# Local-window attention on one Trainium2 core: smaller key tiles, one-pass scores from split operands, and a layer's activations kept in memory

## The chip, the cores and the metric

The kernel runs on one core of one Trainium2 chip. The metric is device time in microseconds (us) of one execution. Each execution of a run also has a span (first to last instruction) and a mean granted TensorE clock. In what follows PE is TensorE, PEld its weight loads, DVE is VectorE, ACT is ScalarE, POOL is GpSimd and SP is SyncE.

## The reference, cut to what matters

Four layers act on four images of 256 channels and 48x48 pixels, each of them with a group norm in front and a residual added. Layers 0 to 2 are convolutions that the change hardly touches. Layer 3 is attention without a softmax: each pixel sums over square windows of 48, 24 and 12 pixels around it.

```python
def _L3_conv_ref(x, Wq, Wk, Wv, Wout, bout):
    # 8 heads of 32 channels, WINDOWS = (1, 2, 4)
    q = sigmoid(einsum('bchw,oc->bohw', x, Wq)); k = sigmoid(... Wk)
    v = v / maximum(norm(v, axis=1), 1e-12)
    for w in WINDOWS:
        ws  = Hh // w
        wk  = _box(Ik, ws, Hh, Ww)        # sums of k over a ws x ws window
        wkv = _box(Ikv, ws, Hh, Ww)       # sums of k v^T over it
        attn = einsum('bdhw,bdfhw->bfhw', q, wkv)
        norm = einsum('bdhw,bdhw->bhw', q, wk)
        outs.append(attn / (norm[:, None] + 1e-06))
    return einsum('bchw,oc->bohw', concatenate(outs), Wout) + bout
...
x = x + _L3_conv_ref(_gn(x), ...)
```

## The kernel before

It computes scores q.k for a tile of 128 key pixels and a block of 8 query rows (384 pixels), multiplies them by a 0/1 mask for each of the three windows, and multiplies the masked scores by v with a column block of ones, so that rows 0 to 31 of an accumulator hold the numerator of a head and rows 32 to 63 its denominator. Two heads are done side by side. A key tile is 128 pixels in a row, that is 2 2/3 rows of the image, and sees all 48 columns.

```python
def attend(qk, vs, rb, ct, pr, o, norm):          # two heads, one block of 8 query rows
    accs = [ps_acc.tile([P, NB], F32, ...) for wi in range(NW)]   # one buffer each
    def scores(kt):
        s = ps_s.tile([P, 2, 512], F32, tag="s")                  # two buffers in all
        for j in range(2):
            g = (2 * pr + j) * D                                  # 32 rows of the array
            nc.tensor.matmul(s[:, j, 0 : (hi - lo) * W],
                qk["k", ct][g : g + D, kt * P : (kt + 1) * P],
                qk["q", ct][g : g + D, lo * W : hi * W], ...)     # fp32
    ahead = scores(todo[0][0])
    for i, kt in enumerate(todo[0]):
        s = ahead
        ahead = scores(next tile)
        for wi in range(NW):
            sm = smp.tile([P, 2, RB, W], F32, tag="sm")
            nc.vector.tensor_mul(sm[...], s[...], masks[...])     # DVE, line 700
            for j in range(2):
                nc.tensor.matmul(accs[wi][64 * j : 64 * (j + 1), ...],
                    vs[ct][:, kt, 2 * pr + j, :], sm[:, j, 0:n, :], ...)   # line 706
    for wi in range(NW):                                          # end of a head pair
        for j in range(2):
            g = (2 * pr + j) * D
            nc.scalar.copy(o[g : g + D, ct, wi, :], accs[wi][64 * j : 64 * j + D])
            nc.scalar.activation(norm[g : g + D, wi, :],
                accs[wi][64 * j + D : 64 * j + 2 * D], AF.Identity, bias=eps_sb[g : g + D])
...
for rb in range(NRB):
    for ct in range(NCT):
        for pr in range(HEADS // NCT // 2):
            attend(qk, vs, rb, ct, pr, o, norm)
            ...                                     # the previous block's output product
        nc.vector.reciprocal(norm, norm)            # line 761: 128 x 1152, all on DVE
        nc.vector.tensor_mul(o[:, ct], o[:, ct], norm)
```

The order of instructions on an engine is not quite that of the source: a scheduler orders them when the program is built.

## Time and profile before

| | before |
|---|---|
| time, median of the first 3 runs | 6971.76 us (6965.56 to 6979.1) |
| profiled span | 6986.8 us |
| mean granted clock | 0.905 |
| last convolution product of layer 2 ends | 2570 us |
| first score of layer 3 | 2660 us |

The page's busy times, groups, stretches and timeline are shown in the prediction below and are not repeated. Two lines of it matter later and were not shown there. They are groups of instructions, with count, then busy us and mean ns, then idle time of the engine just before them:

```profile
L718 ACT ACTIVATE norm<-acc,eps_sb 32x384 f32<-32x384 f32 x576 | 330.3, 573 | 7.2
L717 ACT COPY o<-acc 32x384 f32<-32x384 f32 x576 | 270.3, 469 | 3534.9 <-PE acc L706 3529.8
```

They are the evictions of the accumulators at the end of each of 96 head pairs: 12 small ScalarE operations, each of 32 of 128 partitions, 6.3 us in a row by their means. The accumulators have one buffer each, so the next head pair's products wait for them.

The granted clock over the span in 40 slices (in tenths; 9 is 0.9 or more) shows where the clock is lost. It is mostly layer 3, which begins in slice 15 of 40 (mean 0.87 from 2600 us on); slices 14 and 15 lie largely in layer 2:

```profile
PEclk9999999999999889988889988888898888988888
```

### The profile page before, as it was taken

What the parts mean: (1) busy time and instruction counts of PE and PEld (TensorE: products, weight loads), DVE (VectorE), ACT (ScalarE), POOL (GpSimd) and SP (SyncE); (2) the same over time, 40 slices, a digit from 0 to 9 for tenths busy, and PEclk for the clock granted to TensorE, in tenths of its full rate; (3) what the DMA queues carried; (4) which work ended last, traced back from release to release, by engine and by line L of the source; (5) the groups of instructions that cost most, each with busy time, mean ns of one, the idle gap of its engine ahead of it and who ended that gap; (6) DMA issues with size and microseconds to landing.
All of it is one profiled execution on the core that took longest, in us unless ns stands there. A gap on an engine that the chain in (4) does not pass through costs nothing.

```text
span 6986.8 us, 63861 instructions
## 1 busy us (share of the span) xinstructions
PE 6467.4 (93%) x27732; PEld 2934.3 (42%) x27732; DVE 3257.0 (47%) x4210; ACT 841.5 (12%) x1687; POOL 72.4 (1%) x146
## 2 busy tenths in 40 slices
PE   7999999999999879899989999989899999999998
PEld 3555555455555544333334333334333334333333
DVE  1201110101010216766666776666776665777666
ACT  0000000000000002111112111112111112111111
POOL 0000000000000000000000000000000000000000
PEclk9999999999999889988889988888898888988888
DMA  2000000000000120000000000000000000000000
GB/s 104 9 9 9 7 29 8 6 15 25 5 11 16 9 60 14 5 5 5 5 5 19 5 5 5 5 5 19 5 5 5 1 5 5 10 3 3 5 5 5
DMA packets 100436, 84.81 MB, mean 12 GB/s; under 512 B 70043, under 2 KB 94651, under 8 KB 96443
## 3 DMA queue, kind: packets, MB, share of 16 engines
q1 hardware_dynamic: 89595, 59.85, 3.6%
q10 hardware_dynamic: 10416, 17.44, 0.7%
q0 software_dynamic: 144, 3.43, 0.2%
q8 instruction: 218, 3.57, 0.2%
q14 instruction: 63, 0.52, 0.0%
HBM read 61.37 MB, written 22.75 MB: 12 GB/s over the span
## 4 chain that ended last, share of the span: by engine, by line
PE 88%; DVE 6%; ACT 3%; issue 2%; DMA 2%; SPq 0%; POOL 0%; POOLq 0%; ACTq 0%; DVEq 0%
PE acc L706 29%; PE cv L339 22%; PE s L675 18%; PE cv L462 10%; DVE norm L761 3%; PE out_ps L734 3%; DVE sm L700 2%; PE proj_ps L599 2%; ACT norm L718 1%; PE ap L442 1%; ACT o L717 1%; PE v_ps L621 1%; DMA xn<-x_d 0%; DMA w_sb<-in_w_dram 0%; PE sum_ps L295 0%
## 5 line engine op out<-in xcount | busy, mean ns | idle before, releaser
L700 DVE TENSOR_TENSOR sm<-s,masks 128x768 f32<-128x768 f32 (+7 forms) x3152 | 2439.4, 819 | 1083.6 <-PE s L675 1060.4
L706 PE MATMUL acc<-sm,v 128*64 128x384 f32 (+7 forms) x12608 | 2290.7, 492 | 364.1 <-DVE sm L700 295.6
L706 PEld LDWEIGHTS acc<-sm,v 128*64 128x64 f32 x12608 | 838.4, 148 | 1934.0 <-issue 1114.6
L339 PE MATMUL cv<-pad,w_sb 128*128 128x480 f32 (+1 forms) x3920 | 1579.6, 561 | 0.2 <-DVE pad L318 0.2
L675 PE MATMUL s<-q,k 32*128 32x384 f32 (+5 forms) x5760 | 1448.5, 572 | 10.9 <-DVE sm L700 10.9
L339 PEld LDWEIGHTS cv<-pad,w_sb 128*128 128x128 f32 x3920 | 737.4, 190 | 790.2 <-issue 731.1
L675 PEld LDWEIGHTS s<-q,k 32*128 32x128 f32 x5760 | 501.8, 204 | 660.3 <-issue 610.5
L462 PE MATMUL cv<-pad,wl_sb 128*128 128x384 f32 (+1 forms) x2592 | 712.1, 438 | 4.6 <-DVE pad L176 3.2
L717 ACT COPY o<-acc 32x384 f32<-32x384 f32 x576 | 270.3, 469 | 3534.9 <-PE acc L706 3529.8
L363 DVE TENSOR_TENSOR e<-lg,bn_inv 120x196 f32<-120x196 f32 (+1 forms) x20 | 7.2, 358 | 967.7 <-PE lg L360 967.7
L462 PEld LDWEIGHTS cv<-pad,wl_sb 128*128 128x128 f32 x1728 | 327.3, 190 | 234.4 <-issue 5.5
L761 DVE RECIPROCAL norm<-norm 128x1152 f32<-128x1152 f32 x48 | 352.7, 7347 | 46.5 <-ACT norm L718 46.5
L718 ACT ACTIVATE norm<-acc,eps_sb 32x384 f32<-32x384 f32 x576 | 330.3, 573 | 7.2
L499 DVE SCALAR_TENSOR_TENSOR x<-cv,alpha,x 128x384 f32<-128x384 f32 x48 | 29.6, 617 | 527.5 <-PE cv L462 527.5
L348 ACT ACTIVATE k<-cv,b_sb 128x480 f32<-128x480 f32 (+1 forms) x20 | 12.9, 645 | 2050.4 <-PE cv L339 2050.4
L734 PE MATMUL out_ps<-o,wout_sb 128*128 128x384 f32 x576 | 223.6, 528 | 14.8 <-DVE o L762 14.1
L164 DVE COPY gn_m<-gn_ps 128x2 f32<-128x2 f32 x16 | 2.5, 157 | 371.9 <-PE gn_ps L163 371.6
L734 PEld LDWEIGHTS out_ps<-o,wout_sb 128*128 128x128 f32 x576 | 106.7, 198 | 112.1 <-issue 40.6
L442 PEld LDWEIGHTS ap<-seen,xT 120*128 120x128 f32 (+2 forms) x832 | 115.7, 219 | 18.4 <-ACT seen L435 11.5
L452 DVE TENSOR_TENSOR x<-x,ap 128x240 f32<-128x240 f32 (+1 forms) x80 | 27.0, 391 | 197.7 <-PE ap L442 197.7
L442 PE MATMUL ap<-seen,xT 120*128 120x120 f32 (+3 forms) x832 | 117.5, 304 | 1.1 <-ACT seen L435 0.8
L462 PEld LDWEIGHTS <-wl_sb 128*128 128x128 bf16 x864 | 87.0, 101 | 65.3 <-issue 10.5
(108 smaller groups left out, 1316.7 us busy)
## 6 DMA issues: line engine op xcount, KB each, us to landing
rows<-band_d SPq DMA_DIRECT2D x64, 168.8 KB, 3.0
x<-in_x_dram SPq DMA_DIRECT2D x8, 1152.0 KB, 7.7
x_d<-x SPq DMA_DIRECT2D x8, 1152.0 KB, 4.1
res<-x_d SPq DMA_DIRECT2D x24, 384.0 KB, 3.2
xn<-x_d SPq DMA_DIRECT2D x8, 1152.0 KB, 7.4
out_dram<-res ACTq DMA_DIRECT2D x24, 384.0 KB, 2.5
w_sb<-in_w_dram ACTq DMA_DIRECT2D x14, 448.0 KB, 6.3
masks<-in_masks_dram POOLq DMA_DIRECT2D x1, 3348.0 KB, 25.9
```

Source lines behind the costliest of these rows:

```text
L339: nc.tensor.matmul(ps, w1_sb[:, ct, t, :], pad[:, ct, :, r0 : r0 + nr, c0 : c0 + HP], start=(n == 0), stop=(n == NCT * T0 - 1),)
L442: nc.tensor.matmul(pf[:, f, a:e], xTs[k + i][:n, f, mo * P : (mo + 1) * P], seen[:n, 1 + i, a:e], start=(i == 0), stop=(i == near[-1]),)
L462: nc.tensor.matmul(ps, w_sb[:, ct, t, mo * P : (mo + 1) * P], pad[:, ct, r0 : r0 + RB, c0 : c0 + W], start=(n == 0), stop=(n == NCT * T1 - 1),
L599: nc.tensor.matmul(ps, proj[name][:, ct, mo * P : (mo + 1) * P], xf[:, ct, rb * NB : (rb + 1) * NB], start=(ct == 0), stop=(ct == NCT - 1),)
L621: nc.tensor.matmul(ps, xf[:, ct, kt * P : (kt + 1) * P], proj["v"][:, ct, :], start=(ct == 0), stop=(ct == NCT - 1),)
L675: nc.tensor.matmul(s[:, j, 0 : (hi - lo) * W], qk["k", ct][g : g + D, kt * P : (kt + 1) * P], qk["q", ct][g : g + D, lo * W : hi * W], sta ...
L700: nc.vector.tensor_mul(sm[:, :, 0:n, :], s[:, :, (a - lo) * W : (z - lo) * W].rearrange("p j (r w) -> p j r w", w=W), masks[:, ph, at : at ...
L706: nc.tensor.matmul(accs[wi][64 * j : 64 * (j + 1), (a - rb * RB) * W : (z - rb * RB) * W], vs[ct][:, kt, 2 * pr + j, :], sm[:, j, 0:n, :], ...
L717: nc.scalar.copy(o[g : g + D, ct, wi, :], accs[wi][64 * j : 64 * j + D])
L718: nc.scalar.activation(norm[g : g + D, wi, :], accs[wi][64 * j + D : 64 * j + 2 * D], AF.Identity, bias=eps_sb[g : g + D],)
L734: nc.tensor.matmul(ps, wout_sb[:, kt, mo * P : (mo + 1) * P], o[:, kt % NCT, kt // NCT, :], start=(kt == 0), stop=(kt == NW * NCT - 1),)
L761: nc.vector.reciprocal(norm, norm)
```

## The change

Its intent: make the scores cheaper (each q and k is split into a high and a low half, the four combinations are stacked in 128 rows, and one float32r product replaces a true fp32 one), make the windows tighter (a key tile is 8x16 pixels, so the small windows need only part of the columns), take the wide reciprocal apart (numerators and denominators go through memory, so 24 reciprocals of 128x72 replace 48 of 128x1152), and let the projections of the next image run in the background. In windows where a part of the mask is all ones, ScalarE copies that part and VectorE multiplies the rest.

```diff
+F32R = mybir.dt.float32r
+KC = P // RB                       # 16 columns: key tiles of 8x16 pixels
...
+kst = [kvp.tile([P, NKT, P], F32R, ...) for i in range(2 * NPR)]   # k: high, low, high, low
...
+nc.gpsimd.tensor_copy(hl[:, 0], t)                                  # high half
+nc.gpsimd.tensor_sub(hl[:, 1], t, hl[:, 0].bitcast(F32))            # low half
+nc.sync.dma_start(out=dst[...], in_=hl.bitcast(F32))                # q, k, v to memory
...
 def scores(a, c):
     for j in range(2):
         nc.tensor.matmul(
             s[:, j, 0 : (r1 - r0) * (c1 - c0)],
-            qk["k", ct][g : g + D, kt * P : (kt + 1) * P],
-            qk["q", ct][g : g + D, lo * W : hi * W],
+            kst[2 * pr + j][:, a * NKC + c, :],
+            qs[:, j, r0:r1, c0:c1],
...
+    pieces = [(c0, c1, True)]
+    if abs(a - rb) * RB + RB <= h:
+        f0, f1 = max(0, c * KC + KC - h), min(W, c * KC + h + 1)
+        if f0 < f1:
+            pieces = [(f0, f1, False), (c0, f0, True), (f1, c1, True)]
+    for p0, p1, masked in pieces:
+        if masked:
+            nc.vector.tensor_mul(dst, src, mask[wi][...])            # line 807
+        else:
+            nc.scalar.copy(dst, src)                                 # line 815
...
-            nc.scalar.copy(o[g : g + D, ct, wi, :], accs[wi][64 * j : 64 * j + D])
-            nc.scalar.activation(norm[g : g + D, wi, :], accs[wi][...], AF.Identity, bias=...)
+    if (a, c) == todo[wi][-1]:
+        nc.scalar.copy(stage[:, wi, :], accs[wi])                    # 128 rows at once
+nc.gpsimd.dma_start(out=o_d[b][rb, ...], in_=stage[...])             # and to memory
+nc.gpsimd.dma_start(out=n_d[b][rb : rb + 1, ...], in_=stage[...])
...
-        nc.vector.reciprocal(norm, norm)
-        nc.vector.tensor_mul(o[:, ct], o[:, ct], norm)
+    nc.vector.reciprocal(nr, nr)                                     # 128 x 72
```

The cut parts are the mask tables, the projections in blocks of rows, and the loop that runs the late steps (reciprocal, reload, output product) and the next image's projections between key tiles.

## The prediction

> **What bounds it now.** I read the page's busy times first, then its costliest groups, then the table of 20 us stretches over image 1's attention, then the timeline inside one stretch. The change touches layer 3 alone, which runs from about 2600 to 6987 us: 4387 us of the span.
>
> ```profile
> PE 6467.4 (93%) x27732; PEld 2934.3 (42%) x27732; DVE 3257.0 (47%) x4210; ACT 841.5 (12%) x1687; POOL 72.4 (1%) x146
> ...
> L700 DVE TENSOR_TENSOR sm<-s,masks 128x768 f32<-128x768 f32 (+7 forms) x3152 | 2439.4, 819 | 1083.6 <-PE s L675 1060.4
> L706 PE MATMUL acc<-sm,v 128*64 128x384 f32 (+7 forms) x12608 | 2290.7, 492 | 364.1 <-DVE sm L700 295.6
> ...
> L675 PE MATMUL s<-q,k 32*128 32x384 f32 (+5 forms) x5760 | 1448.5, 572 | 10.9 <-DVE sm L700 10.9
> ...
> L761 DVE RECIPROCAL norm<-norm 128x1152 f32<-128x1152 f32 x48 | 352.7, 7347 | 46.5 <-ACT norm L718 46.5
> ```
>
> PE is nearly always busy, and DVE waits for PE, not PE for DVE. That names PE, but a busy PE may be a slow one. The stretches (columns: stretch, length, PE, PEld, DVE, ACT, POOL, PE clock, DMA share, GB/s) show when:
>
> ```profile
> 4320.00:4340.00 20.00, 20.00 (x122) 8.09 (x122) 18.18 (x23) 0.16 (x1) 0.00 (x0) 1.00 0.00 1
> 4340.00:4360.00 20.00, 11.68 (x62) 4.45 (x62) 15.01 (x11) 6.08 (x12) 0.00 (x0) 0.88 0.00 1
> 4360.00:4380.00 20.00, 20.00 (x64) 6.34 (x64) 8.06 (x11) 0.00 (x0) 0.00 (x0) 0.50 0.00 0
> 4380.00:4400.00 20.00, 20.00 (x114) 7.98 (x112) 15.96 (x21) 1.30 (x3) 0.00 (x0) 0.94 0.00 1
> ```
>
> PE idles 8 us, then runs 20 us at half clock, issuing 64 matmuls instead of about 120. The timeline there names the cause:
>
> ```profile
> 4349.87 7.35 DVE L761 RECIPROCAL norm<-norm 128x1152 f32<-128x1152 f32 x1
> ...
> 4358.09 1.54 PE L706 MATMUL acc<-sm,v 128*64 128x384 f32 x4 [6.69 <-DVE sm L700]
> ```
>
> The wide reciprocal stands in front of the mask products, so PE waits 6.69 us. This happens 48 times. The third thing to read is a stretch without it:
>
> ```profile
> 4082.88 0.91 PE L675 MATMUL s<-q,k 32*128 32x384 f32 x4
> 4083.72 1.92 PE L706 MATMUL acc<-sm,v 128*64 128x384 f32 x12
> 4085.57 0.91 PE L675 MATMUL s<-q,k 32*128 32x384 f32 x4
> 4086.41 1.76 PE L706 MATMUL acc<-sm,v 128*64 128x384 f32 x12
> 4088.10 0.91 PE L675 MATMUL s<-q,k 32*128 32x384 f32 x4
> ```
>
> From start to start, a score group takes 0.84 us and the acc groups 1.85 and 1.69 us. Their windows have 1008 and 912 columns in the source, so 0.16 us buys 96 columns: 1.67 ns per column of a pair of heads, the two heads side by side. What is left is a fixed 0.17 us for an acc group and, at 384 columns, 0.20 us for a score group. The same two constants fit other steps.
>
> **The sum of layer 3 before**, at full clock. Counts come from the built program: scores 1,027,584 columns / 2 x 1.67 = 856 us; acc 2,022,912 / 2 x 1.67 = 1686; output, q/k and v products 221,184 x 1.67 = 369; 2917 changes of group x 0.18 = 525. That is 3436 us. The other 951 us are the reciprocals and what follows them (48 x about 17 = 800: 7 of idling, 10 lost at half clock), and some 150 us around the four projections.
>
> **What the skill says.** (1) "FP8 and Floating Point Precision", TensorE Precision Notes: true FP32 makes four passes through the array, reduced-precision FP32 is truncated to FP22. 1.67 ns is four cycles at the 2.4 GHz of "TensorE: Matmul & The Clock Gate", so the four passes agree; one pass for float32r no run here shows. (2) "TensorEngine Tiling (Array Packing)", Key Properties: "Changing tiling mode (not just tile) drains the TensorE". The trace agrees: 0.17 to 0.20 us at each change between 32-row and 64-column tiles. After the change scores use the whole array and acc still 64-column tiles, so this cost stays. (3) "TensorE: Matmul & The Clock Gate", the HAM clock gate: an idle window of about 3.4 us drops the clock to half. The trace agrees on 0.50, but it stays there some 20 us here. (4) "DMA: Bandwidth & Descriptors", Anatomy of one DMA: about 2.0 us fixed for a software DMA. The kernel before has one such issue, of 3348 KB (25.9 us), which doesn't test it.
>
> **The change, part by part.**
> - *Scores.* Four 32-row copies (k high/low by q high/low) fill 128 rows, so one pass replaces four, but the heads no longer run side by side. Tiles of 8x16 pixels see at most 40 columns at the edges: 970,752 columns x 0.417 ns = 404 us instead of 856. Gain 452.
> - *Acc.* 1,716,800 columns instead of 2,022,912: 1431 us, gain 255. In the new order 226 products stand apart from their partner; half of them pay again, about 0.5 us each: +57.
> - *Changes of mode* 3310 x 0.18 = 596: +71. Output and projections unchanged, 369.
> - *DVE.* A product costs about 1.04 ns per element plus 0.105 us (2439 us for 3152 products with 2,022,912 elements). Now 4032 products, 1,171,520 elements: 1220 + 423 = 1643 us. The wide reciprocals become 24 of 72 columns. With o<-o,rc (48 x 1.35), evictions and small ops: some 1820 us, against 2857 of PE.
> - *ACT* gets 1440 unmasked copies (0.3 to 0.6 us, estimated from the 0.47 us of a 384-column copy and the 0.58 us of a 512-column one), 288 stage copies, sigmoids and table loads: about 1000 us.
> - *Projections* of images 1 to 3 run as background between steps. The first stays in front, and GpSimd now does its normalising and splitting: at the 525 ns of a 128x240 copy in this trace, some 13 us per row block, 80 us for six. With writing q/k/v out and reading k/v back: 115 us, where PE's share (already counted) is 30 to 45. I book +85, and +30 for the last output's trip through memory.
>
> PE in layer 3: 404 + 1431 + 57 + 596 + 369 = 2857 us. By step: the central tile of a near row block takes PE 1.84 us plus 0.37, DVE 1.73; an edge tile 1.47 + 0.37 against 1.35; far tiles 0.8 to 1.2 + 0.37 against 0.7 to 0.9. PE stays ahead in each kind, by 0.4 us or more, so it remains the bound.
>
> **New waits.** 24 times DVE meets two operations that need memory: the small reciprocal, about 10 us of DVE work after the heads end, behind four software DMAs, a write and a read; and o<-o,rc, about 8 us later, behind a write and eight more DMAs. I estimate 4 us each, 190 us in all. GpSimd's queue holds DMA issues and projection work in one line; 18 row blocks late by 4 us: 70 us. Low clock after some of these: 100 us. Waits: 360.
>
> Total: 2575 + 2857 + 85 + 30 + 360 = 5907; I say **5900 us**, 15% less.
>
> **Rivals.**
> - *float32r isn't one pass*, or its weight loads show: two passes would add 404 us (6300). Loads of 0.19 us, as now for 128 fp32 columns, would stick out of a 320-column product of 0.13 us: +86. For it: nothing in this trace has the type. Against: the high/low stacking makes sense only with one pass.
> - *Waits for memory replace the reciprocal's.* If all 48 cost what the reciprocal cost (17 us with the low clock), 800 us are given back: 6350 to 6700. For it: DVE takes its work in order, and one late operation blocks all masks. Against: two attends' work lies around each, and the program places them late.
> - *DVE or ACT becomes the bound*, with only two score buffers released by both. By sums no (64% and 35% of PE); small stalls of 10% in each step would make 6150.
> - *All waits hidden*: 5550.
>
> **Range and chances.** 5550 to 6350 holds the hidden case and the two-pass case. To lose the 2% gain, waits would have to eat over 900 us beyond my 360: 0.02 slower, 0.02 same, 0.96 faster.
>
> **What would show it.** Score groups: one record per product of about 0.13 to 0.16 us, a pair in 0.45 to 0.55 us with its change of mode; twice that speaks for the first rival. DVE busy in layer 3 near 1800 us, no operation over 2 us. Clock in layer 3 above 0.93, not 0.86; stretches at 0.5 beginning where DVE waits for nr or rc would show the second rival. PE waiting for DVE or ACT for over 300 us without a DMA behind it would show the third. The prediction fails if the score or mode-change constants don't carry over, or if GpSimd, not PE, sets the pace.

## The result, and the profile after

The changed kernel is correct and took 5853.32 us (median of 4 runs, 5849.97 to 5857.83) against 6974.2 us before (4 runs, 6965.56 to 6979.1). The ratio is 0.8394, 95% interval 0.838 to 0.8409. A ratio here is the mean time of one kernel's runs over that of the other's runs of the same rounds, so it is not quite the ratio of the medians that are quoted.

The page of the kernel after: busy times, and the clock in slices.

```profile
PE 5535.8 (95%) x25684; PEld 2763.7 (47%) x25684; DVE 2169.4 (37%) x5202; ACT 1075.7 (18%) x2179; POOL 732.0 (13%) x1193
...
PEclk9999999999999999889999999999999999999998
```

The low clock is gone from layer 3, except at its start (0.77 to 0.80 during the first projection). The mean over the whole span is 0.982. The costliest groups of the same page:

```profile
L807 DVE TENSOR_TENSOR sm<-s,masks 128x240 f32<-128x240 f32 (+22 forms) x4032 | 1689.0, 456 | 1120.6 <-PE s L765 687.9
L817 PE MATMUL acc<-sm,vst 128*64 128x320 f32 (+14 forms) x13440 | 1985.9, 398 | 120.7 <-DVE sm L807 104.3
...
L815 ACT COPY sm<-s 128x528 f32<-128x528 f32 (+3 forms) x1440 | 690.7, 486 | 1601.9 <-DVE sm L807 1587.8
L765 PE MATMUL s<-qs,kst 128*128 128x320 f32 (+3 forms) x2880 | 838.6, 374 | 9.6 <-DVE sm L807 8.6
```

The scores are now 2880 products of one record each, where they were 5760 records. Busy time of overlapping matmul records is not their cost, so starts are read from the timeline (start, length, engine, line, operation, count, and the idle time before with its releaser). This is a stretch of image 1's attention after the change; "..." stands for weight loads:

```profile
3763.15 0.56 PE L765 MATMUL s<-qs,kst 128*128 128x320 f32 x2
...
3763.64 1.14 PE L817 MATMUL acc<-sm,vst 128*64 128x224 f32 x8
3764.29 0.29 ACT L815 COPY sm<-s 128x144 f32<-128x144 f32 x1 [1.10 <-DVE sm L807]
3764.62 0.52 DVE L807 TENSOR_TENSOR sm<-s,masks 128x240 f32<-128x240 f32 x2 [0.36 <-ACT sm L815]
...
3764.71 0.62 PE L765 MATMUL s<-qs,kst 128*128 128x384 f32 x2
3765.23 0.48 ACT L815 COPY sm<-s 128x384 f32<-128x384 f32 x1 [0.64 <-DVE sm L807]
...
3765.26 1.16 PE L817 MATMUL acc<-sm,vst 128*64 128x168 f32 x12
```

A pair of scores takes 0.49 us from start to start at 320 columns and 0.55 us at 384. That is 0.417 ns per column of a head, plus 0.227 us per pair, so float32r is one pass. The second thing to see: ScalarE waits for VectorE, then VectorE for ScalarE, then ScalarE for VectorE again, although over layer 3 (2552 to 5851 us) VectorE is busy for only 56% of the time and ScalarE for 29%. The waits of layer 3's attention after the change (engine, line, what it waited for: us in total, times, longest us) have it at large:

```profile
ACT sm L815 <- DVE sm L807: 1574.8, 1126, 9.5
...
DVE sm L807 <- ACT sm L815: 411.7, 891, 2.0
...
PEld acc L817 <- DVE sm L807: 309.9, 897, 7.7
...
PE acc L817 <- DVE sm L807: 100.1, 194, 7.4
...
DVE nr L848 <- DMA nr<-n_d: 17.4, 3, 8.4
...
DVE o L874 <- DMA rc<-r_d: 1.0, 1, 1.0
```

VectorE waited 411.7 us for ScalarE, and 18.4 us for memory.

**Where the time went.** For every group of consecutive PE products of one kind I took the time from its start to the start of the next group, subtracted the columns at 0.417 ns (float32r) or 1.67 ns per pair of heads (fp32), and a fixed cost per group (the median where nothing waits: 0.20 us before and 0.227 us after for scores, 0.16 us for acc, 0.20 us for the others). What remains is called excess: waiting, work at a low clock, and products that find no partner to run beside them. Stretches: 2690 to 6986 us before, 2700 to 5810 us after.

| us | before | after | difference |
|---|---|---|---|
| score columns | 851 | 403 | -448 |
| acc columns | 1674 | 1424 | -250 |
| other products | 316 | 306 | -10 |
| fixed cost of groups (number) | 532 (2909) | 654 (3401) | +122 |
| excess at low clock (under 0.97) | 778 | 36 | -742 |
| excess at full clock | 131 | 283 | +152 |
| sum | 4282 | 3105 | -1177 |

So 698 us came from fewer and cheaper columns, and 742 us from the clock; 122 us were given back by group changes, and 152 us by more excess at full clock.

Not all of this excess is waiting. The columns were counted as if every acc product of one head ran beside one of the other head. A product has two records, so a group in which all have a partner has a multiple of four. After the change 226 acc groups do not, as here (x10 and x6):

```profile
3699.95 1.55 PE L817 MATMUL acc<-sm,vst 128*64 128x162 f32 x10
3701.43 0.56 PE L765 MATMUL s<-qs,kst 128*128 128x320 f32 x2
3701.93 1.39 PE L817 MATMUL acc<-sm,vst 128*64 128x312 f32 x6
```

In the first group the last product of 320 columns runs alone. These 226 groups hold 72 of the 283 us, so some 210 us are waiting. Before, 98 score groups of this kind hold 69 of the 131 us, part of it waiting. The first projection takes longer, too: from the last convolution to the first score it is 131 us instead of 90.

### The profile page after: what moved, and what is told of

It reads as the page before. It is cut to its first block, busy times and chain, and to the rows that moved or that the text cites. A ratio compares the mean times of both kernels' runs of the same rounds, so it can differ in the third digit from the quotient of the medians. Undisturbed runs are those within 1.5% of the kernel's fastest.

```text
span 5851.2 us, 65381 instructions
## 1 busy us (share of the span) xinstructions
PE 5535.8 (95%) x25684; PEld 2763.7 (47%) x25684; DVE 2169.4 (37%) x5202; ACT 1075.7 (18%) x2179; POOL 732.0 (13%) x1193
## 4 chain that ended last, share of the span: by engine, by line
PE 82%; DVE 6%; issue 4%; DMA 4%; POOL 3%; ACT 1%; SPq 0%; DVEq 0%; POOLq 0%; ACTq 0%
PE cv L334 27%; PE acc L817 25%; PE cv L457 12%; PE s L765 11%; DVE sm L807 4%; PE out_ps L879 3%; PE proj_ps L635 2%; PE ap L437 1%; DVE o L874 1%; POOL xn L621 1%; DMA nr<-n_d 1%; PE proj_ps L674 1%; DMA o_d<-stage 0%; POOL sq L683 0%; ACT sm L815 0%
## 5 line engine op out<-in xcount | busy, mean ns | idle before, releaser
L807 DVE TENSOR_TENSOR sm<-s,masks 128x240 f32<-128x240 f32 (+22 forms) x4032 | 1689.0, 456 | 1120.6 <-PE s L765 687.9
L817 PE MATMUL acc<-sm,vst 128*64 128x320 f32 (+14 forms) x13440 | 1985.9, 398 | 120.7 <-DVE sm L807 104.3
L817 PEld LDWEIGHTS acc<-sm,vst 128*64 128x64 f32 x13440 | 762.0, 136 | 851.6 <-issue 405.1
L815 ACT COPY sm<-s 128x528 f32<-128x528 f32 (+3 forms) x1440 | 690.7, 486 | 1601.9 <-DVE sm L807 1587.8
L765 PE MATMUL s<-qs,kst 128*128 128x320 f32 (+3 forms) x2880 | 838.6, 374 | 9.6 <-DVE sm L807 8.6
L765 PEld LDWEIGHTS s<-qs,kst 128*128 128x128 f32 x2880 | 436.1, 189 | 742.7 <-issue 694.8
L831 POOL DMA_DIRECT2D o_d<-stage x192 | 96.9, 505 | 1312.0 <-ACT sm L815 1055.9
L827 ACT COPY stage<-acc 128x384 f32<-128x384 f32 x288 | 137.8, 479 | 484.5 <-PE acc L817 479.6
L387 POOL COPY flat<-pad 128x240 f32<-128x240 f32 (+1 forms) x80 | 34.6, 460 | 1516.8 <-PE trx L400 1480.8
L674 PE MATMUL proj_ps<-wv_sb,xn 128*128 128x256 f32 x288 | 96.6, 441 | 20.2 <-ACT sg L652 12.6
```

The source lines that it names most:

```text
L674: nc.tensor.matmul(ps, xn[:, ct, c, :], proj["v"][:, ct, :], start=(ct == 0), stop=(ct == NCT - 1),)
L765: nc.tensor.matmul(s[:, j, 0 : (r1 - r0) * (c1 - c0)], kst[2 * pr + j][:, a * NKC + c, :], qs[:, j, r0:r1, c0:c1], start=True, stop=True,)
L807: nc.vector.tensor_mul(dst, src, mask[wi][:, mr : mr + n, mc : mc + p1 - p0] .unsqueeze(1) .to_broadcast([P, 2, n, p1 - p0]),)
L815: nc.scalar.copy(dst, src)
L817: nc.tensor.matmul(accs[wi][64 * j : 64 * (j + 1)].rearrange("p (r w) -> p r w", w=W)[:, r0:r1, c0:c1], vst[pr][:, a * NKC + c, j, :], sm[ ...
L827: nc.scalar.copy(stage[:, wi, :], accs[wi])
```

## The experiments

Three questions were open. Was it the reciprocal that cost 800 us before? What is the waiting among the 283 us at full clock after? Is a change of kind of product really a price per change? Theory for the second: two engines read one score tile, and are made to take turns. Rivals: memory, or VectorE's amount of work. All ratios are against the kernel before on the same chip (6962 to 6970 us there). The change itself was timed in another round, in which the kernel before took 6974 us, so a difference to its 5853 us is uncertain by some 10 us: the ratios give 198, 241, 187 and 186 us for the 190, 250, 194 and 196 us below.

### Before, without the reciprocal

```diff
-                    nc.vector.reciprocal(norm, norm)
+                    nc.vector.tensor_scalar_add(norm, norm, 0.0)
```

The result is wrong on purpose.

> The kernel before, with the wide reciprocal replaced by a plain add of 0 over the same 128x1152 tile (the result is wrong on purpose; everything else is as it was). My account says that the 48 reciprocals cost layer 3 about 800 us, 350 of them idle PE and the rest half clock after it, so 6974 should become about 6170 to 6250, with the clock in layer 3 back from 0.86 to 0.97 or more. The rival account, in which scores at a quarter of the passes and fewer columns are the main gain of the change (707 us of 1121), leaves 400 us for the reciprocals: about 6570.

Measured: 6412.1 us (6410.92 to 6417.24), ratio 0.9212, clock 0.961. The reciprocals cost 550 us (6962.4 - 6412.1), between the two expectations and 250 us short of the prediction's 800. (The add that stands in their place takes 0.755 us of VectorE, 48 times, so this is the cost beyond such an add.) By the same bookkeeping, 219 us of excess at low clock and 139 us at full clock remained. The timeline of this run at the end of a head pair (without weight loads) shows what was left:

```profile
4338.85 0.47 ACT L717 COPY o<-acc 32x384 f32<-32x384 f32 x1 [29.34 <-PE acc L706]
...
4339.33 0.57 ACT L718 ACTIVATE norm<-acc,eps_sb 32x384 f32<-32x384 f32 x1
...
4342.08 0.87 PE L706 MATMUL acc<-sm,v 128*64 128x384 f32 x4 [1.05 <-ACT norm L718]
...
4344.22 2.83 PE L706 MATMUL acc<-sm,v 128*64 128x384 f32 x8 [1.27 <-ACT norm L718]
```

The evictions run from 4338.85 to 4345.24, one after the other, and PE waits for them twice. Each wait is under 1.3 us, and the clock still falls: by the trace's clock records at 4343.18 us, that is after the first wait and 0.2 us into the second. The table of 10 us stretches of the same run (stretch, length, PE, PEld, DVE, ACT, POOL, clock, DMA share, GB/s):

```profile
4340.00:4350.00 10.00, 7.67 (x32) 2.76 (x32) 5.83 (x7) 5.11 (x10) 0.00 (x0) 0.66 0.01 2
4350.00:4360.00 10.00, 10.00 (x28) 2.69 (x28) 3.67 (x5) 0.00 (x0) 0.00 (x0) 0.50 0.00 0
4360.00:4370.00 10.00, 10.00 (x38) 4.00 (x36) 5.07 (x8) 0.00 (x0) 0.00 (x0) 0.50 0.00 0
4370.00:4380.00 10.00, 10.00 (x60) 3.78 (x56) 7.86 (x9) 1.07 (x3) 0.00 (x0) 0.98 0.01 2
```

PE is idle for 2.3 us of one stretch and then works at half clock for over 20 us (27.3 us by the clock records). This is one of the long cases: of the 45 stretches of low clock in this run from the first score on, 28 last 3.4 us and 8 over 20 us. What decides their length was not settled.

### Before, with the reciprocal in twelve pieces

```diff
-                    nc.vector.reciprocal(norm, norm)
+                    for wi in range(NW):
+                        for c0 in range(0, NB, NB // 4):
+                            nc.vector.reciprocal(norm[:, wi, c0 : c0 + NB // 4], ...)
```

> The kernel before, with each 128x1152 reciprocal cut into twelve of 96 columns; DVE's work stays the same or grows a little (12 x some 0.7 us), but no single block of 7.3 us stands before the masks. If it is the length of the block that idles PE and drops its clock, most of the 800 us come back: 6200 to 6450. If it is DVE's total work, or the scheduler still puts the pieces in a row, nothing changes: 6900 to 7000.

Measured: 6594.06 us (6593.18 to 6612.45), ratio 0.9478, clock 0.947, correct. It gains 368 us of the 550, between the two expectations. PE still waits for the mask products behind the pieces (188 us), because the scheduler often puts several pieces in a row. It says that the same work hurts less in pieces; it doesn't settle more.

### Before, without the end of a head pair

```diff
-                for j in range(2):
-                    nc.scalar.copy(o[g : g + D, ct, wi, :], accs[wi][64 * j : 64 * j + D])
-                    nc.scalar.activation(norm[g : g + D, wi, :], accs[wi][...], AF.Identity, ...)
+                nc.scalar.copy(o[:, ct, wi, :], accs[wi])
...
-                    nc.vector.reciprocal(norm, norm)
-                    nc.vector.tensor_mul(o[:, ct], o[:, ct], norm)
```

The result is wrong on purpose.

> The kernel before without the reciprocals, without the product o<-o,norm and with 3 ScalarE copies of 128 rows per head group instead of 12 of 32 rows (result wrong on purpose). Without the reciprocals alone it took 6412 us and still had 358 us beyond streaming and fixed costs. Theory (the rest of the prediction's 800 us is the end of each head group, where 12 evictions of 0.47 to 0.57 us hold the accumulators): 6090 to 6200 us and a clock above 0.975. Rival (the rest sits around the projections): 6320 to 6400 us.

Measured: 6197.08 us (6189.15 to 6204.27), ratio 0.8902, clock 0.985. The theory's range and clock are met. The whole end of a head pair was worth 765 us (6961.9 - 6197.1), 550 for the reciprocal and 215 for nine of the twelve evictions, the product after them and the add that had replaced the reciprocal (the run does not tell these apart). In its bookkeeping, excess at low clock is 38 us and at full clock 92.

### After, with fp32 scores again

```diff
-                        kst[2 * pr + j][:, a * NKC + c, :],
-                        qs[:, j, r0:r1, c0:c1],
+                        kst[pr][D * j : D * (j + 1), a * NKC + c, :],
+                        qs[D * j : D * (j + 1), r0:r1, c0:c1],
```

The splitting into halves and the four copies go too; q and k are stored once, in fp32.

> The changed kernel with the float32r scores undone: q and k stay one fp32 tile each, scores are plain fp32 products of 32-row tiles, two heads side by side, as before the change; tiles of 8x16, masks, output path stay changed. PE's score time rises from 404 to 809 us, its fixed part falls by 33: +372 us of PE work. If PE alone set the pace of the steps: 5853 + 372 = 6225. If the 340 us that PE waits inside the steps come from DVE and ACT taking turns on a score tile, the longer scores hide part of that wait: +150 to +280, 6000 to 6130.

Measured: 6043.73 us (6036.02 to 6046.31), ratio 0.8679, correct. In the new order the one-pass scores are worth 190 us, and not the 397 us by which their columns differ (800 - 403, by the bookkeeping). There are 62 us less for changes of group without them, and the excess falls from 319 to 184 us: a slower PE gives the two vector engines time. So part of the gain on the scores went into waits. A smaller part went into the splitting: without it the first score comes 110 us after the last convolution, and not 131.

### After, without ScalarE copies

```diff
-                    if abs(a - rb) * RB + RB <= h:
+                    if False:
```

Every window is one masked VectorE product again. The result stays right, since the mask is one where ScalarE had copied.

> The changed kernel with no unmasked copies on ACT: every window is one masked product on DVE (3360 instead of 4032 products, 1.717 million elements instead of 1.172). DVE's work rises from 1690 to about 2140 us, but it no longer hands the score tile to ACT and back. My theory (PE's 340 us of small waits come from that turn-taking): waits shrink, 5650 to 5800. Rival (DVE's amount of work is what PE waits for): slower than 5853, 5950 to 6200.

Measured: 5602.66 us (5602.29 to 5604.7), ratio 0.8048, correct: 250 us faster than the change, a little more than expected, and far from the rival. From the page of this run, the mask products and the acc products:

```profile
L807 DVE TENSOR_TENSOR sm<-s,masks 128x640 f32<-128x640 f32 (+18 forms) x3360 | 2111.2, 683 | 490.9 <-PE s L765 480.2
L817 PE MATMUL acc<-sm,vst 128*64 128x320 f32 (+14 forms) x13440 | 1844.0, 393 | 39.0 <-DVE sm L807 29.4
```

VectorE does 422 us more mask work (2111.2 against 1689.0), and PE waits less for it. By the bookkeeping, the excess falls from 319 to 93 us.

This run changes two things, though: one engine instead of two, and fewer instructions. The next two take them apart.

### After, same pieces, all on VectorE

```diff
                         else:
-                            nc.scalar.copy(dst, src)
+                            nc.vector.tensor_copy(dst, src)
```

> The changed kernel with each ScalarE copy made a VectorE copy of the same piece: the same 5472 pieces, but one engine reads a score tile, so no hand-over. VectorE gets some 600 us more work than after the change, by the 0.3 to 0.5 us of such a piece. Theory (hand-over): 5590 to 5690 us, near the 5603 of the version with one product per window. Rival (what cost time was the number of pieces, or VectorE's amount of work): 5800 to 5950 us.

Measured: 5659.51 us (5654.35 to 5662.12), ratio 0.8126, correct. From its page:

```profile
L807 DVE TENSOR_TENSOR sm<-s,masks 128x240 f32<-128x240 f32 (+23 forms) x4032 | 1689.3, 451 | 451.3 <-PE s L765 438.7
...
L815 DVE COPY sm<-s 128x528 f32<-128x528 f32 (+3 forms) x1440 | 778.9, 541 | 0.0
```

The same 5472 pieces, with 779 us of copies moved onto the busier engine, run 194 us faster than on two engines. VectorE's amount of work is not the cause; sharing the tile between two engines is. By the bookkeeping the gain has two parts. Only 12 acc groups instead of 226 have a product without a partner, which takes their excess from 72 to 4 us; the rest of the excess, mostly waiting, falls from 247 to 129 us. So the scheduler's order, which differs between the two runs, is a part of it. A run of the change with PE's order held fixed would separate order from hand-over in full; it was not made. The 57 us between this run and the one before it are the price of the extra pieces.

### After, ScalarE's copies of a key tile before VectorE's products

```diff
+                for on_act in (True, False):
+                    for wi, r0, r1, c0, c1, pieces, sm in work:
                         for p0, p1, masked in pieces:
+                            if p0 == p1 or masked == on_act:
+                                continue
```

Both engines keep their work, but they take turns on a tile once, and not once for each window.

> The changed kernel with the ScalarE copies of a key tile issued before all VectorE products of that tile, so that the two engines take turns on a score tile once instead of once per window; same instructions, same work. Theory (the hand-overs between two readers of one score tile are the 250 us that the version without ScalarE copies gained): at least half of it comes back, 5640 to 5740 us, and VectorE's wait for ScalarE falls from 412 us to under 200. Rival (ScalarE is too slow or VectorE starts too late, so the order doesn't matter): 5800 to 5900 us.

Measured: 5656.84 us (5651.56 to 5673.02), ratio 0.8127, correct: in the theory's range, 196 us faster than the change. One half of the expectation missed. VectorE's wait for ScalarE did not fall; it is now

```profile
DVE sm L812 <- ACT sm L820: 854.0, 861, 4.9
...
PEld acc L824 <- DVE sm L812: 313.0, 867, 4.5
...
ACT sm L820 <- DVE sm L812: 216.0, 162, 1.4
```

(waits of this run's attention). VectorE waits longer in sum, but ScalarE no longer waits for VectorE (1126 times before, 162 now). So going to and fro within a tile is what cost time, by one way or another; waiting once at its start seems to be hidden behind PE. By the bookkeeping this gain, too, is not all waiting: the source now puts all acc products of a tile after its pieces, and there are 3211 groups instead of 3401 (33 us less fixed cost) and 18 acc groups with a product alone instead of 226 (5 us instead of 72). The rest of the excess falls from 247 to 149 us.

### After, without copies, and the first projection partly on VectorE

```diff
-                        nc.gpsimd.tensor_scalar(            # normalise, low half, scale v
+                        eng.tensor_scalar(                  # eng: nc.vector for image 0
```

> The changed kernel without ScalarE copies (5603 us before) and with image 0's normalising, low-half subtraction and v scaling on VectorE instead of GpSimd. Theory (GpSimd sets the pace of the first projection, some 148 us where TensorE has 35): 30 to 70 us off, 5530 to 5575 us. Rival (transfers to memory or TensorE's own waits set it): 5590 to 5610 us.

Measured: 5587.19 us (5584.19 to 5594.79), ratio 0.8024, correct. The first score comes at 2660 us instead of 2676, so the gain is 16 us, half of the least that was expected; the time lies between the two ranges. GpSimd was only part of what held the first projection; what else does was not settled. This is the fastest version. It beats the kernel before by 19.8%, and the change by some 260 us.

### Scores ahead across head pairs

```diff
+                elif next_job is not None:
+                    ahead.append(scores(next_job, next_job[5][0]))
```

> The version without ScalarE copies and with the first projection partly on VectorE (5587 us), with the first scores of the next head pair issued ahead of the last key tile's acc products, as within a head pair. Its trace has 94 us of excess over streaming and fixed costs in the attention. Theory (much of it is the empty start of each of 96 head pairs): 30 to 70 us off, 5515 to 5560 us. Rival (it sits elsewhere): 5575 to 5600 us.

Measured: 5602.45 us (5595.52 to 5607.73), ratio 0.8038 (0.8026 to 0.805), correct. A miss: no gain. The bookkeeping's excess stayed (94 us before, 92 after), so the start of a head pair is not where it sits. Where it sits is open.

### Key tiles two at a time

```diff
-            groups = [tiles[n : n + 1] for n in range(0, len(tiles), 1)]
+            groups = [tiles[n : n + 2] for n in range(0, len(tiles), 2)]
```

> The same with key tiles taken two at a time: the scores of two tiles in a row, then the acc products of two tiles, so that 720 score groups and 720 acc groups replace 1440 each; 12 instead of 7 product buffers; same arithmetic. Theory (0.227 us for a score group and 0.16 us for an acc group are the price of each change between whole-array and 64-column products, paid per group): 720 x 0.387 = 279 us off the version with one tile at a time, 5240 to 5340 us. Rival 1 (the 0.227 us belongs to the products, by their weight loads of 0.189 us): only 115 us off, 5400 to 5450 us. Rival 2 (with only two score tiles, TensorE waits for VectorE): 5500 us or more, with waits of acc and s for the products of line sm.

Measured: 5648.88 us (5647.79 to 5650.31), ratio 0.8105, correct. The run tests nothing: the scheduler had broken up the pairs, and the trace has 3027 groups instead of some 1900. So the order was held by a dependency without a semaphore from each score or acc product to the one before it, in a version with one tile at a time as a control, and in one with two.

```diff
+        def link(inst):            # called on every score and acc product
+            if last:
+                tc.add_manual_dep(inst.ins, last[0].ins.name, <NoSync>, reason="order")
+            last[:] = [inst]
```

> The version that issues scores ahead across head pairs (5602 us), with the TensorE order of scores and acc products held to the order in the source, one key tile at a time: products of two heads stay side by side, and the background products come in between. Control for the next run; 5550 to 5610 us, and some 3200 groups instead of 3331.

Measured: 5604.54 us (5597.75 to 5606.8), ratio 0.8039, correct, with 3351 groups, not some 3200. Holding the order costs nothing against the version before it.

> Key tiles two at a time as in a_pairs, whose order the scheduler had broken up (3027 groups instead of some 1900), with the order now held: two tiles' scores, then two tiles' acc products. Theory (0.227 and 0.16 us are paid per change between whole-array and 64-column products): up to 720 x 0.387 = 279 us off a_chain, 5290 to 5380 us. Rival 1 (0.227 us belongs to each score pair by its weight loads of 0.189 us): 5440 to 5500 us. Rival 2 (with two score tiles in all, VectorE comes late in the heavy row blocks): over 5500 us, with waits of acc and s for VectorE of over 150 us.

Measured: 5627.43 us (5619.08 to 5632.0), ratio 0.8077, correct, clock 0.960. By its time this is rival 2. But the theory's term is right too: there are 1820 groups instead of 3351, to which the bookkeeping gives a fixed cost of 358 us instead of 646, 288 us less (that the cost goes with the group is read from the starts below). The excess rose from 87 to 388 us, of which 185 lie at low clock. The timeline of PE shows both:

```profile
3726.84 0.86 PE L782 MATMUL s<-qs,kst 128*128 128x320 f32 x4
3727.64 2.85 PE L833 MATMUL acc<-sm,vst 128*64 128x168 f32 x24
3730.42 0.97 PE L782 MATMUL s<-qs,kst 128*128 128x384 f32 x4
...
3742.16 0.54 PE L782 MATMUL s<-qs,kst 128*128 128x320 f32 x2 [1.35 <-DVE sm L819]
3743.86 0.98 PE L782 MATMUL s<-qs,kst 128*128 128x384 f32 x2 [1.16 <-DVE sm L819]
```

Four score products of 320 columns take 0.80 us from start to start: 4 x 133 ns of columns and 0.26 us. Two took 0.49 us, with 0.227. So the fixed cost is paid per change and not per product; the weight loads of 189 ns lie behind the products. The starts of single products say more. Of the 0.227 us, 0.119 stand between the first score product and the second, and 0.108 between the last one and the acc product; in groups of four the products in between start 0.150 us apart, of which 0.133 are columns. Where a product of the whole array (128*128) follows a pair of scores, as it does 31 times after the change, the 0.108 us are 0.014: that part is the price of going over to 64-column tiles. But there are two score tiles in all, and both are now held until VectorE has read them. PE waits for VectorE at the heavy row blocks (188 us in sum for the scores), and its clock falls after such waits (here at 3743.31 us; 309 us at low clock from the first score on, 107 with one tile at a time). A gain on one engine was eaten by a wait of the same size.

## Why the prediction was right or wrong

The predicted 5900 us were within 47 us of the measured 5853, and inside the range. Its steps:

- **Score and acc columns: right.** Gains of 452 and 255 us were predicted, 448 and 250 us were found. Acc took its columns at the old rate, scores at a quarter of it, in one record per product.
- **Changes of group: right in kind, somewhat small.** 71 us more were predicted for the number of changes, 122 found: 3401 groups instead of 3310, and the constant of 0.18 us is 0.227 for float32r scores (0.16 for acc). That it is a price per change was shown only by the version with tiles two at a time. The 57 us for 226 products apart from their partner were right: 226 groups, 72 us, which the table has under excess at full clock.
- **The old waits: right in sum, wrong in their owner.** The step "951 us are the reciprocals and what follows them (48 x about 17 = 800), and some 150 us around the four projections" has 909 us of excess in the trace. The whole end of a head pair was 765 us, near the 800. But the reciprocals were 550 of it, and 215 were mostly the evictions and the product after them, which the prediction did not name. That part mattered: the kernel with the reciprocal alone taken out still lost clock. The change also made 3 evictions of 12 and put the product at another place, and 36 us at low clock are left; which of the two did more was not tested. I had read one 6.69 us wait and put the whole end of a head pair down to it.
- **The new waits: too large, and wrong in kind.** 360 us were booked: 190 for memory, 70 for late row blocks, 100 for low clock. Some 247 us were found (the 319 us of excess without the 72 us of products alone), 211 of them at full clock. VectorE waited 18.4 us for memory, not 190; excess at low clock was 36 us. That the total still came near is luck: a wait that was not booked stood in for two that did not come. The late row blocks were not measured apart. The step that failed is the dismissal of the third rival, "By sums no (64% and 35% of PE)": no engine was the bound by its sum, and the waits came all the same, by the turns of two engines on one tile. The rival's own sign, "PE waiting for DVE or ACT for over 300 us without a DMA behind it", is in the profile only with PE's weight loads (309.9 us; its products waited 100.1 us), and it is a poor sign: it was there before the change (658.8 us), and the run with ScalarE's copies first, which is 196 us faster, still has 313.0 us of it. A weight load can wait while products still stream. What is shown is by the runs: with the pieces on one engine, or with one hand-over for each tile, 194 and 196 us come back. About 120 and 100 us of this are waits by the bookkeeping, some 67 us in each are products that have a partner again. The rest of the waits is not accounted for.
- **This was to be known beforehand.** The Trainium skill, "PSUM — Partial Sum Buffer", section "PSUM bank collisions raise a hardware error", states that two engines may not access the same bank and quadrant at the same time, two readers included, and that the compiler's scheduler adds a dependency between any two instructions on different engines that do, "reads and writes alike". A score tile of 2 x 512 floats is two banks, one for each head, and both engines read both. The traces agree with the ordering (1126 waits of ScalarE for VectorE and 891 the other way); no run here tried the collision itself. The prediction's section on the skill looked at passes, tiling, clock and DMA, and at none of the PSUM rules, although the diff sets a second reader on a PSUM tile.
- **First projection and tail: right enough.** 115 us were booked for the first projection; from the last convolution to the first score it is 131. The tail from the last acc product (5808) to the end (5851) is 43 us, near the 30 above PE's share. That GpSimd sets the pace there (80 us for six row blocks) is only partly borne out: moving its largest items gained 16 us. The prediction's sums are not quite of a piece here: layer 3 begins at 2600 us in the sum before, and the total is built on 2575. The last convolution ends at 2570 us before and 2552 after, which helped by some 20 us.
- **VectorE and ScalarE: right.** About 1820 and 1000 us were predicted for layer 3; between 2552 and 5851 us they are busy for 1846 and 945 us, at a mean clock of 0.98 (over 0.93 had been asked for). The reciprocals are now 594 ns, 24 of them, against 7347 ns, 48 of them.
- **float32r rival: refuted.** One pass, and the weight loads don't show. The one-pass scores are worth 190 us and not 397 less 62, mainly because waits grew with PE's speed.

## What to carry to other kernels

Before work on a PSUM tile is shared out between two engines, ask who reads that tile: here the two took turns, and a tile that went to and fro was slower than the same pieces on one engine, even though this engine then had far more to do. If both are to read it, group each engine's share so that the tile changes hands once. Look at the order of products too: in the version with the shared tile, more products that could run side by side stood apart. When a wait at the end of a step is large, list everything that stands there, and take the pieces out one at a time: here the wide reciprocal hid twelve narrow evictions, and shorter waits than the longest were enough to lose the clock. And a cost removed from the bounding engine is a gain only as far as its buffers let it run on.

## What the Trainium skill lacked or had wrong

- "TensorE: Matmul & The Clock Gate", section "Part 1: The HAM clock gate": the page gives about 3.4 us of idling to lose the clock, and as long to get it back. Here a wait of 1.05 us and 0.23 us of a second one were enough, and half clock then lasted 27.3 us of full work (of 45 low stretches in that run from the first score on 28 lasted 3.4 us, as on the page, and 8 over 20 us). The page does say that the window runs free; it gives no length for shorter idling that is enough.
- "TensorEngine Tiling (Array Packing)", section "Key Properties": it says that a change of tiling mode drains the engine, and gives no cost. Here a change costs 0.16 us for an acc group and 0.227 us (pair of scores) to 0.26 us (four scores) for a score group, paid per group; the last 0.108 us of a score group, before 64-column products, are 0.014 when a product of the whole array follows.
- "FP8 and Floating Point Precision", section "TensorE Precision Notes": it has four passes for true fp32, and no number of passes for float32r. Here it is one: 0.417 ns per column, and a weight load of 128 columns, 189 ns, hides: products of 320 columns (133 ns) in a row start 150 ns apart.
- No page that I found gives the time of a wide VectorE reciprocal: 7347 ns for 1152 fp32 elements per partition and 594 ns for 72.
- "PSUM — Partial Sum Buffer" has the rule that mattered, but no price: with two engines on one score tile in turns, 5853 us; with the same pieces on one engine, 5660 us (some 67 us of the difference being products that have a partner again).
